# Rank order, rank widths and the last rank's evacuation in a fused cross-attention and mixture-of-experts kernel

## The chip, the cores and the metric

The kernel runs on one core of a Trainium2 chip. The metric is the device time of one execution in microseconds (us).

## What is computed

The input is 2048 tokens (4 x 512) of width 512, all in f32. The first half of the reference adds to each token a gated block chosen by its token id; the change doesn't touch it. The second half is a mixture of experts:

```python
logits = jnp.einsum('th,eh->te', x, gate_w)
topk_w, topk_ids = jax.lax.top_k(softmax(logits), K)       # K = 4 of E = 32
topk_w = topk_w / jnp.sum(topk_w, axis=-1, keepdims=True)
...
gu = jnp.einsum('ech,ehf->ecf', buf, w13)                  # 512 -> 2 x 256
g, u = jnp.split(gu, 2, axis=-1)
act = jax.nn.silu(g) * u
eo = jnp.einsum('eci,eih->ech', act, w2)                   # 256 -> 512
routed = jnp.zeros_like(x).at[tok].add(out_slots * flat_w[order][:, None])
...
out = residual + (routed + shared).reshape(B, S, Hd)
```

Here `x` is the normalised input, `buf` gathers the tokens of each expert, and `shared` is a further gated block that all tokens pass. An expert has 256 tokens on average; how many each one has follows from the data.

## The kernel before, in words

**Until about 257 us.** The tokens go through the first half in blocks of 128. Each token's row (512 values, 4 expert numbers, 4 weights, its own number) is scattered by GpSimd into a table in DRAM, `s_dram`, which has 320 slots for each expert. The shared block follows in four groups of 512 tokens (`glu_up` L848, `shared` L876); its results and the residual are put into `out` by GpSimd. Meanwhile `ranks()` (L791) counts the tokens of each expert and sorts the experts by count: rank 0 has the most. It also works out `over`: whether any expert has more tokens than its rank may have (`lim`, L827 to L841). If so, a slow branch after the loop (L1297) redoes the work; its condition is loaded by each engine at L1263.

**The expert loop (L1249 to L1293).** It runs over `ORDER`, a list of the 32 ranks written out by hand; I call a position in it a place, 0 to 31. Each place computes up to 256 tokens of its rank (`CM`). Ranks 0 to 5 may have 64 more tokens, ranks 6 to 17 may have 32 more; these extra rows of two ranks (64 each) or four ranks (32 each) are packed to 128 rows and computed together, as a block, at the place of the first of these ranks (0, 2, 4, 6, 10, 14). Ranks from `LOW` on compute fewer than 256 columns (`width`, L1057).

At a place:

- Sync's queue fetches rows three places ahead (`fetch` L961, `fetch_x` L970 for a block) and weights five places ahead (`weights` L921, six DMAs of 256 KB). There are six sets of weight buffers, so a place's weights may be loaded once the place six before is done with its own.
- DVE transposes the rows (L993) and scales them (L999, ACT L1003).
- `up_rank` (L1063) multiplies by `w13`: 16 matmuls whose moving operand is as wide as the rank, into `pg` and `pu`; then silu on ACT (L1076) and the product on DVE (L1079). Where a rank is narrower than 256, DVE sets the rest of `aT` to zero (L1087).
- If a block is due, `up_block` (L1154), `turn_block_act` (L1174) and `down_block` (L1182) run its matmuls, L1161, L1177 and L1188.
- `down_rank_by_halves` (L1098) multiplies by `w2` with seven products of halves (L1114) in place of eight. ACT (L1117) and DVE (L1120) weight and combine them into `eo`, two tiles of 128 rows. The last rank uses the plain `down_rank` (L1143) with `weighted` (L1035).
- `push` (L1040): GpSimd adds each tile of `eo` to the rows of `out` that its tokens own, by an indirect DMA that accumulates. The adds of one expert touch different rows and are declared free of each other. Two experts may share tokens, so the first add of a place waits until all adds of the place before have landed. A place whose rank has extra rows has a third add (`eo_x`).

At place 29 a drain is put into GpSimd's queue behind the adds of place 28 (L1259 to L1261). PSUM pools: `ps_o` and `ps_t` have two buffers each, `ps_m` three, `ps_s` one. `eo` has seven buffers.

The tile framework may interleave instructions of neighbouring places on PE: the up products of the next place run between the seven products of this one.

Of the kernel before, what the change touches and what calls it, by code (L numbers as in the profile page):

```python
# [8 lines left out]
F32 = mybir.dt.float32  # L9
I32 = mybir.dt.int32  # L10
U32 = mybir.dt.uint32
AF = mybir.ActivationFunctionType
ALU = mybir.AluOpType
AX = mybir.AxisListType
# [3 lines left out]
P = 128  # L18
T = 2048
D = 512  # L20
# [6 lines left out]
E = 32  # L27
K = 4
C = 2 * T * K // E
CM = 256  # L30
MJ = CM // P
I = 256
IC = I // P
# [4 lines left out]
XA, XWA = 6, 64  # L38
XZ, XWB = 18, 32
# [1 line left out]
NXA = XA // XPA  # L41
NX = NXA + (XZ - XA) // XPB

LOW = ((26, 240), (29, 228))


ORDER = (
    [0, 1, 2, 3, 18, 19]
    + [*range(6, 10), 20, 21, 4, 5, 22, 23]
    + [*range(10, 14), 24, 25]  # L50
    + [*range(14, 18), *range(26, E)]
)
SL = CM + XWA
NS = E * SL
# [12 lines left out]
def tile_xattn_moe(  # L67
# [15 lines left out]
    nc = tc.nc  # L83

    const = ctx.enter_context(tc.tile_pool(name="const", bufs=1))
# [3 lines left out]
    ps_t = ctx.enter_context(tc.tile_pool(name="ps_t", bufs=2, space=PSUM))  # L89
    ps_m = ctx.enter_context(tc.tile_pool(name="ps_m", bufs=3, space=PSUM))  # L90
    ps_o = ctx.enter_context(tc.tile_pool(name="ps_o", bufs=2, space=PSUM))
# [112 lines left out]
    def behind(ins, other, kind=mybir.DependencyClass.NoSync):  # L204

        tc.add_manual_dep(
            ins.ins,
            other.ins.name,
            mybir.DependencyInfo(kind, mybir.DependencyReason.DATA),
            reason="order",  # L210
        )
# [21 lines left out]
    n = EX * NT  # L233
# [546 lines left out]
    def base(j):  # L780
        return put_rows(out, xtok[:, j : j + 1], acc[:, j, :], out_puts, "base")
# [9 lines left out]
    def ranks():  # L791
        pn = ps_s.tile([P, E], F32, tag="sm", name="pn")
        nc.tensor.matmul(pn, ones16, before_[G], start=True, stop=True)
        n_e = slots.tile([P, E], F32, name="n_e")
        nc.vector.tensor_copy(n_e, pn)
        key = slots.tile([P, E], F32, name="key")
        nc.vector.scalar_tensor_tensor(key, n_e, float(E), iota_e, ALU.mult, ALU.subtract)
        grid = slots.tile([P, E, E], F32, tag="grid", name="grid")
        nc.vector.tensor_tensor(
            grid,  # L800
            key.unsqueeze(1).to_broadcast([P, E, E]),
            key.unsqueeze(2).to_broadcast([P, E, E]),
            ALU.is_gt,
        )
        rank = slots.tile([P, E], F32, name="rank")
        nc.vector.tensor_reduce(rank, grid, AX.X, ALU.add)

        def of(ranks_, n, name):

            pick = grid[:, :n, :]  # L810
            nc.vector.tensor_tensor(
                pick,
                ranks_.unsqueeze(2).to_broadcast([P, n, E]),
                rank.unsqueeze(1).to_broadcast([P, n, E]),
                ALU.is_equal,
            )
            nc.vector.tensor_tensor(pick, pick, iota_e.unsqueeze(1).to_broadcast([P, n, E]), ALU.mult)
            er = const.tile([P, n], F32, name=name)
            nc.vector.tensor_reduce(er, pick, AX.X, ALU.add)
            return er  # L820

        er = of(iota_e, E, "er")
        er_i = const.tile([P, E], I32, name="er_i")
        nc.vector.tensor_copy(er_i, er)
        er_x = of(rank_x, NX, "er_x")

        lim = slots.tile([P, E], F32, name="lim")  # L827
        more = slots.tile([P, E], F32, name="more")
        nc.vector.tensor_scalar(lim, rank, float(XA), float(XWA - XWB), ALU.is_lt, ALU.mult)
        nc.vector.tensor_scalar(more, rank, float(XZ), float(XWB), ALU.is_lt, ALU.mult)  # L830
        nc.vector.scalar_tensor_tensor(lim, lim, float(CM), more, ALU.add, ALU.add)
        had = CM
        for r, n in LOW:
            nc.vector.tensor_scalar(more, rank, float(r), float(had - n), ALU.is_ge, ALU.mult)
            nc.vector.tensor_tensor(lim, lim, more, ALU.subtract)
            had = n
        nc.vector.tensor_tensor(lim, n_e, lim, ALU.is_gt)
        over = slots.tile([P, 1], F32, name="over")
        nc.vector.tensor_reduce(over, lim, AX.X, ALU.add)
        over_i = const.tile([P, 1], I32, name="over_i")  # L840
        nc.vector.tensor_copy(over_i, over)  # L841
        return er, er_x, er_i, over_i


    HD = D // 2
    muls_s, adds_s = [], []

    def glu_up(xT, w13t, name):  # L848
        aT = cols.tile([P, IC, GT * P], F32, tag="aT", name=f"aT_{name}")
        for f in range(IC):  # L850
            pg = ps_m.tile([P, GT * P], F32, tag="mm", name="pg")
            pu = ps_m.tile([P, GT * P], F32, tag="mm", name="pu")
            for ps, fo in ((pg, f), (pu, IC + f)):
                for c in range(DC):
                    ins = nc.tensor.matmul(
                        ps, w13t[:, c, fo * P : (fo + 1) * P], xT[:, c, :], start=(c == 0), stop=(c == DC - 1)
                    )
                    if c % 2:
                        step(ins)
            if f == 0:  # L860
                first_half = ins
            s = mid.tile([P, GT * P], F32, tag="silu", name="s")
            nc.scalar.activation(s, pg, AF.Silu)
            muls_s.append(nc.vector.tensor_tensor(aT[:, f, :], s, pu, ALU.mult))
        return aT, first_half

    def glu_down(aT, w2t, i):
        po = ps_o.tile([P, D], F32, tag="po", name="po")
        for f in range(IC):
            ins = nc.tensor.matmul(  # L870
                po, aT[:, f, i * P : (i + 1) * P], w2t[:, f, :], start=(f == 0), stop=(f == IC - 1)
            )
        step(ins)
        return po

    def shared(g, aT):  # L876
        for i in range(GT):
            j = g * GT + i
            po = glu_down(aT, shw2, i)
            adds_s.append(nc.vector.tensor_tensor(acc[:, j, :], acc[:, j, :], po, ALU.add))  # L880
            to_put.append(lambda j=j: base(j))
# [27 lines left out]
    wts_a = ctx.enter_context(tc.tile_pool(name="wts_a", bufs=2))  # L909
    third = ctx.enter_context(ExitStack())  # L910
    slots = third.enter_context(tc.tile_pool(name="slots", bufs=1))
    er, er_x, er_i, over_i = ranks()
    for g in range(G):
        if g:
            aT_s[g], _ = glu_up(h2T[g], shw13, f"s{g}")
        shared(g, aT_s[g])
    while to_put:
        to_put.pop(0)()

# [113 lines left out]
    EO = 7  # L1033

    def weighted(po, wt, name, tag, m=P):  # L1035
        eo = last.tile([P, D], F32, tag=tag, name=f"eo_{name}", bufs=EO if tag == "eo" else 2)
        nc.scalar.mul(eo[:m, :], po[:m, :], wt[:m, :])
        return eo
# [18 lines left out]
    def width(r):  # L1057

        return min([CM] + [n for r_, n in LOW if r >= r_])

# [82 lines left out]
    def down_rank(aT, w2t, wt, to, n, r):  # L1143
        for j in range(MJ):
            m = min(P, n - j * P)
            po = ps_o.tile([P, D], F32, tag="po", name="po")
            for f in range(IC):
                nc.tensor.matmul(
                    po[:m, :], aT[:, f, j * P : j * P + m], w2t[:, f, :], start=(f == 0), stop=(f == IC - 1)
                )  # L1150
            eo = weighted(po, wt[:, j : j + 1], f"{r}_{j}", "eo", m)
            push(eo[:m, :], to[:m, j : j + 1], f"rank{r}")

    def up_block(xT, ws, name, after_=None, turned_=None):  # L1154
# [68 lines left out]
    wt = {r: weights(r) for r in ORDER[:2]}  # L1223
# [6 lines left out]
    last = ctx.enter_context(tc.tile_pool(name="last", bufs=1))  # L1230
# [18 lines left out]
    for i, r in enumerate(ORDER):  # L1249
# [14 lines left out]
        if q is not None:  # L1264
            xT_next, next_ = turn_parts(got[q][0], f"{q}", summed)
        R = w2_sums(wt[r][1], r) if r < E - 1 else None
        aT, made, last_up, wr = up_rank(
            xT,
            wt[r][0],
            width(r),  # L1270
            f"r{r}",
            next_,
            lambda first_: given(got[r][1], er[:, r : r + 1], f"{r}", first_),
        )
# [8 lines left out]
        if pend:  # L1283
            n, rs_, ws, a, xw, tox = pend
            aTx = turn_block_act(a, f"x{n}")
            eo = weighted(down_block(aTx, ws, last_up), xw[:, 0:1], f"x{n}", "eo_x")
            m = P // len(rs_)
# [8 lines left out]
    slots = ctx.enter_context(tc.tile_pool(name="slots_l", bufs=1))  # L1296
    with tc.If(need > 0):  # L1297
# [37 lines left out]
        for q in range(NT // NH):  # L1335
# [5 lines left out]
            for t in range(NH):  # L1341
                j = q * NH + t
# [4 lines left out]
            for e in range(E):  # L1347
                w = weights(e, e)
                for t in range(NH):
                    j, name = q * NH + t, f"l{q}_{e}_{t}"  # L1350
                    xw = given(of_l[:, t : t + 1, :], iota_e[:, e : e + 1], name)
                    a = up_block(rows_l[t], [w], name)
                    po = down_block(turn_block_act(a, name), [w])
# [7 lines left out]
                    eo = last.tile([P, D], F32, tag="eo", name=f"eo_{name}", bufs=EO)  # L1361
                    nc.scalar.copy(eo, po)
                    nc.vector.scalar_tensor_tensor(acc[:, j, :], eo, xw[:, 0:1], acc[:, j, :], ALU.mult, ALU.add)
                    po = ps_o.tile([P, D], F32, tag="po", name="po_l")
# [3 lines left out]
        for j in range(NT):  # L1368
            tp = ps_s.tile([P, P], F32, tag="sm", name="tp_l")
# [3 lines left out]
            po = ps_o.tile([P, D], F32, tag="po", name="po_l")  # L1373
# [4 lines left out]
        for i in range(NT):  # L1378
            nc.vector.tensor_scalar(row_l, xtok, float(-i * P), None, ALU.add)
            po = ps_o.tile([P, D], F32, tag="po", name="po")  # L1380
# [43 lines left out]
```

## Time and profile before

| what | us |
|---|---|
| median of 3 runs (lowest to highest) | 624.11 (622.13 to 624.48) |
| the profiled execution | 623.74 |
| its span | 621.9 |
| first up product of place 0 starts | 257.2 |
| last matmul of the last rank ends | 610.6 |
| last add issued by GpSimd | 614.6 |

A profile row has the line, the engine, the operation, the output and the inputs. A timeline row starts with its start and its length in us; in brackets at its end stand the engine's idle time before it and what ended that. A PE row counts records; each f32 matmul has two of them. The granted clock is 1.00 all through the expert loop. The code lines in the profile are those of the kernel before.

### The profile page before, as it was taken

The numbers are of one execution on the slowest core, as the hardware profiler recorded it, in microseconds if no ns is written. First come the engines' busy times: TensorE is split into PE (matmuls) and PEld (weight loads), VectorE is DVE, ScalarE is ACT, GpSimd is POOL, SyncE is SP. The second block draws the span as 40 slices with busy tenths as digits, with TensorE's granted clock in tenths as the row PEclk, the third lists the DMA queues.
The fourth block names the chain that finished last, engine by engine and source line by source line (L and its number), as shares of the span: only waits on it lengthen the run. The fifth ranks groups of instructions, "written<-read, shape, count | busy, mean of one in ns | idle before, by whom it ended". The sixth has DMA issues, their size and how long they took to land. (4 is left out here: it accounts for less than half of the span.)

```text
span 621.9 us, 10438 instructions
## 1 busy us (share of the span) xinstructions
PE 601.4 (97%) x2962; PEld 433.5 (70%) x2962; DVE 401.1 (65%) x1113; ACT 216.8 (35%) x390; POOL 248.6 (40%) x217
## 2 busy tenths in 40 slices
PE   5999999999999999999999999999999999999992
PEld 2777767777644444567786788768778886888881
DVE  7655456676548611766677677857867776787850
ACT  2445675756332000122233233333333333333330
POOL 4461002266677655332252343243323424243432
PEclk9999999999999999999999999999999999999997
DMA  7489993226365788699989997998999999999434
GB/s 252 155 310 396 414 413 154 104 105 224 122 249 198 271 323 240 211 320 285 306 169 277 281 226 171 293 247 180 253 273 277 193 219 296 264 250 227 52 40 57
DMA packets 104450, 144.55 MB, mean 232 GB/s; under 512 B 21184, under 2 KB 58048, under 8 KB 101824
## 3 DMA queue, kind: packets, MB, share of 16 engines
q1 hardware_dynamic: 86400, 101.54, 55.1%
q0 software_dynamic: 17984, 42.26, 28.1%
q8 instruction: 26, 0.43, 0.3%
q14 instruction: 40, 0.33, 0.2%
HBM read 79.05 MB, written 66.22 MB: 234 GB/s over the span
## 5 line engine op out<-in xcount | busy, mean ns | idle before, releaser
L1042 POOL DMA_INDIRECT out<-eo,to_all x64 | 101.5, 1587 | 221.0 <-DVE eo L1120 92.1
L1072 PE MATMUL pg<-xT,w 128*128 128x256 f32 (+2 forms) x512 | 135.4, 377 | 0.0
L1117 ACT ACTIVATE eo<-po,wt 128x256 f32<-128x256 f32 x124 | 58.6, 474 | 167.0 <-PE po L1114 147.0
L1072 PE MATMUL pu<-xT,w 128*128 128x256 f32 (+2 forms) x512 | 114.0, 376 | 0.0
L1072 PEld LDWEIGHTS pg<-xT,w 128*128 128x128 f32 x512 | 96.6, 190 | 18.5 <-issue 6.2
L1072 PEld LDWEIGHTS pu<-xT,w 128*128 128x128 f32 x512 | 97.3, 190 | 11.5
L652 POOL DMA_INDIRECT s_dram<-h,slot x64 | 64.1, 1002 | 24.4 <-issue 15.2
L464 PEld LDWEIGHTS pp<-xT,held 128*128 128x128 f32 x576 | 66.8, 192 | 7.4 <-issue 5.7
L464 PE MATMUL pp<-xT,held 128*128 128x128 f32 x576 | 68.2, 276 | 0.6 <-DVE st_b L611 0.6
L485 PE MATMUL po<-cT,aT 128*128 (+1 forms) x152 | 68.4, 592 | 0.0
L993 DVE STREAM_TRANSPOSE xT<-z 128x1024 f32<-128x1024 f32 x32 | 65.1, 2034 | 0.0
L1120 DVE SCALAR_TENSOR_TENSOR eo<-po,wt,eo 128x256 f32<-128x256 f32 x93 | 44.9, 484 | 24.6 <-PE po L1114 19.6
L1079 DVE TENSOR_TENSOR aT_r<-s,pu 128x256 f32<-128x256 f32 (+2 forms) x64 | 26.5, 414 | 39.0 <-PE pu L1072 37.1
L485 PEld LDWEIGHTS po<-cT,aT 128*128 128x128 f32 x152 | 27.4, 190 | 27.3 <-issue 27.3
L1003 ACT ACTIVATE xT<-xT,nwq 128x256 f32<-128x256 f32 x64 | 29.0, 500 | 46.2 <-DVE xT L993 45.2
L618 POOL TENSOR_TENSOR rs<-rs,mhalf 128x2 f32<-128x2 f32 x16 | 11.3, 705 | 72.7 <-DVE rs L617 72.7
L1095 DVE TENSOR_TENSOR t_r<-w,t_r 128x256 f32<-128x256 f32 x62 | 26.4, 426 | 21.0 <-PE po L1114 20.4
L395 ACT COPY held<-cT 128x1024 f32 x36 | 36.0, 1047 | 10.2 <-DVE valid L312 10.0
L1114 PE MATMUL po<-w,aT_r 128*128 128x256 f32 x124 | 37.8, 386 | 0.1
L1114 PE MATMUL po<-t_r,s_r 128*128 128x256 f32 x124 | 37.6, 385 | 0.0
L1114 PE MATMUL po<-t_r,aT_r 128*128 128x256 f32 x124 | 37.3, 382 | 0.0
L870 PE MATMUL po<-shw,aT_s 128*128 128x512 f32 x64 | 29.6, 602 | 0.3 <-DVE acc L880 0.3
(203 smaller groups left out, 763.5 us busy)
## 6 DMA issues: line engine op xcount, KB each, us to landing
w<-in_w SPq DMA_DIRECT2D x192, 256.0 KB
s_dram<-none SPq DMA_DIRECT2D x1, 20840.0 KB
z<-s_dram SPq DMA_DIRECT2D x128, 128.0 KB
h_dram<-h SPq DMA_DIRECT2D x4, 1042.0 KB
cT<-in_ctxT SPq DMA_DIRECT2D x4, 1024.0 KB
out<-none SPq DMA_DIRECT2D x1, 1024.0 KB
s_dram<-h,slot POOLq DMA_INDIRECT x64, 3.3
out<-eo,to_all POOLq DMA_INDIRECT x64, 7.3
```

The lines of the kernel that those rows point to most:

```text
L395: ins = nc.scalar.copy(held[b][:, h : h + n], cT[:, bass.ds(e, 1), h : h + n].rearrange("p o c f -> p (o c) f"))
L464: ins = nc.tensor.matmul(ups[b][:, f, :], held[b][:, c, f * P : (f + 1) * P], xT_[b][:, c, :], start=(f == 0 and c == 0) if b == 0 else (c ...
L485: ins = nc.tensor.matmul(po, aT_[b][:, f, :], cT[:, bass.ds(off[b], 1), f, :].rearrange("p o f -> p (o f)"), start=(f == 0), stop=(f == DC ...
L652: put = nc.gpsimd.indirect_dma_start(out=table, out_offset=bass.IndirectOffsetOnAxis(ap=index, axis=0), in_=src, in_offset=None,)
L870: ins = nc.tensor.matmul(po, aT[:, f, i * P : (i + 1) * P], w2t[:, f, :], start=(f == 0), stop=(f == IC - 1))
L993: ins = nc.vector.transpose(xT.rearrange("p c (r b) -> p r c b", b=SQ), z.rearrange("p r (a c) -> p r c a", c=DC))
L1003: on_act.append(nc.scalar.mul(xT[:, c, :], xT[:, c, :], nwq[:, c : c + 1]))
L1042: put = nc.gpsimd.indirect_dma_start(out=out, out_offset=bass.IndirectOffsetOnAxis(ap=dst, axis=0), in_=eo, in_offset=None, bounds_check=T ...
L1072: last_up = nc.tensor.matmul(ps, w13t[:, c, f * P : (f + 1) * P], xT[:, c, :n], start=(c == 0), stop=(c == DC - 1))
L1114: return nc.tensor.matmul(ps, L[i], R[i], start=first_, stop=True, skip_group_check=True)
L1117: nc.scalar.mul(eo[i][:, j, :], ps, wt[:, i : i + 1])
L1120: return nc.vector.scalar_tensor_tensor(eo[i][:, j, :], ps, wt[:, i : i + 1], eo[i][:, j, :], ALU.mult, ALU.add)
```

## The change

It has four parts. `LOW` gets more entries: ranks 20 to 25 become narrower than 256 and ranks 28, 30 and 31 narrower than they were. `ORDER` moves ranks 4 and 5, with the block of their extra rows, from places 12 and 13 to 28 and 29; the later ranks of the middle move up. The limits are worked out by a function of their own, behind the adds of the shared block's group 1. The last rank's results are computed in two column halves, each in a PSUM bank of its own, from `ps_o` for the first 128 rows and from `ps_t` for the others; ACT weights the first half and DVE the second.

| places | 0 to 5 | 6 to 9 | 10 to 13 | 14 to 17 | 18 to 21 | 22 to 25 | 26 to 31 |
|---|---|---|---|---|---|---|---|
| before | 0 1 2 3 18 19 | 6 7 8 9 | 20 21 4 5 | 22 23 10 11 | 12 13 24 25 | 14 15 16 17 | 26 27 28 29 30 31 |
| after | 0 1 2 3 18 19 | 6 7 8 9 | 20 21 22 23 | 10 11 12 13 | 24 25 26 14 | 15 16 17 27 | 28 29 4 5 30 31 |

```diff
-LOW = ((26, 240), (29, 228))
+LOW = ((20, 252), (22, 248), (24, 244), (26, 240), (28, 234), (29, 228), (30, 224))
...
     [0, 1, 2, 3, 18, 19]
-    + [*range(6, 10), 20, 21, 4, 5, 22, 23]
-    + [*range(10, 14), 24, 25]
-    + [*range(14, 18), *range(26, E)]
+    + [*range(6, 10), *range(20, 24)]
+    + [*range(10, 14), *range(24, 27)]
+    + [*range(14, 18), *range(27, 30)]
+    + [4, 5, 30, 31]
...
-        lim = slots.tile([P, E], F32, name="lim")
...
-        return er, er_x, er_i, over_i
+        def limits(after_):
+
+            lim = slots.tile([P, E], F32, name="lim")
+            more = slots.tile([P, E], F32, name="more")
+            behind(
+                nc.vector.tensor_scalar(lim, rank, float(XA), float(XWA - XWB), ALU.is_lt, ALU.mult), after_
+            )
...
+            return over_i
+
+        return er, er_x, er_i, limits
...
-    er, er_x, er_i, over_i = ranks()
+    er, er_x, er_i, limits = ranks()
...
         shared(g, aT_s[g])
+        if g == 1:
+            over_i = limits(adds_s[-1])
...
     def down_rank(aT, w2t, wt, to, n, r):
         for j in range(MJ):
             m = min(P, n - j * P)
-            po = ps_o.tile([P, D], F32, tag="po", name="po")
-            for f in range(IC):
-                nc.tensor.matmul(
-                    po[:m, :], aT[:, f, j * P : j * P + m], w2t[:, f, :], start=(f == 0), stop=(f == IC - 1)
-                )
-            eo = weighted(po, wt[:, j : j + 1], f"{r}_{j}", "eo", m)
+            banks, tag = ((ps_o, "po"), (ps_t, "tp"))[j % 2]
+            eo = last.tile([P, D], F32, tag="eo", name=f"eo_{r}_{j}", bufs=EO)
+            for h in range(2):
+                of = slice(h * HD, (h + 1) * HD)
+                po = banks.tile([P, HD], F32, tag=tag, name="po")
+                for f in range(IC):
+                    nc.tensor.matmul(
+                        po[:m, :], aT[:, f, j * P : j * P + m], w2t[:, f, of], start=(f == 0), stop=(f == IC - 1)
+                    )
+                if h:
+                    nc.vector.tensor_scalar(eo[:m, of], po[:m, :], wt[:m, j : j + 1], None, ALU.mult)
+                else:
+                    nc.scalar.mul(eo[:m, of], po[:m, :], wt[:m, j : j + 1])
             push(eo[:m, :], to[:m, j : j + 1], f"rank{r}")
```

More of the change, by code (lines that the diff above doesn't have):

```diff
@@ L825, in ranks @@
         er_x = of(rank_x, NX, "er_x")
-        lim = slots.tile([P, E], F32, name="lim")
[L828 to L841, printed above, removed]
-        return er, er_x, er_i, over_i
+        def limits(after_):
[4 more added lines that the diff above has]
+            )
+            nc.vector.tensor_scalar(more, rank, float(XZ), float(XWB), ALU.is_lt, ALU.mult)
+            nc.vector.scalar_tensor_tensor(lim, lim, float(CM), more, ALU.add, ALU.add)
+            had = CM
+            for r, n in LOW:
+                nc.vector.tensor_scalar(more, rank, float(r), float(had - n), ALU.is_ge, ALU.mult)
+                nc.vector.tensor_tensor(lim, lim, more, ALU.subtract)
+                had = n
+            nc.vector.tensor_tensor(lim, n_e, lim, ALU.is_gt)
+            over = slots.tile([P, 1], F32, name="over")
+            nc.vector.tensor_reduce(over, lim, AX.X, ALU.add)
+            over_i = const.tile([P, 1], I32, name="over_i")
+            nc.vector.tensor_copy(over_i, over)
+            return over_i
+        return er, er_x, er_i, limits
     HD = D // 2
```

## The prediction

> **What bounds the kernel now.** I read the page's busy shares first, then the stretches of the expert loop, then what PE waited for, then GpSimd's timeline.
>
> The page, and the stretches of the expert loop (columns: us, then busy of PE, PEld, DVE, ACT and POOL, granted clock, DMA share, GB/s):
>
> ```profile
> PE 601.4 (97%) x2962; PEld 433.5 (70%) x2962; DVE 401.1 (65%) x1113; ACT 216.8 (35%) x390; POOL 248.6 (40%) x217
> ```
>
> ```profile
> 433.00:480.00 47.00, 47.00 (x241) 36.15 (x240) 34.33 (x82) 14.41 (x30) 15.47 (x10) 1.00 1.11 269
> 522.00:570.00 48.00, 48.00 (x234) 40.01 (x234) 35.80 (x87) 15.99 (x33) 18.92 (x13) 1.00 1.08 262
> 570.00:611.00 41.00, 40.59 (x190) 33.91 (x188) 26.37 (x70) 13.53 (x28) 15.12 (x10) 1.00 0.51 67
> ```
>
> PE is busy without a gap from 257.2 to 610.6 us at full clock, so TensorE work taken off the loop shortens it one for one. The DMA engines are full as well, until about 570 us, when the last weights are in; then their share halves. PE's waits in the loop are 0.3 us at most. But PE's end isn't the kernel's end: 11.3 us follow. The timeline says why:
>
> ```profile
> 392.01 1.55 POOL L1042 DMA_INDIRECT out<-eo,to_all  x1 [5.85 <-DVE wt L1022]
> 393.86 1.55 POOL L1042 DMA_INDIRECT out<-eo,to_all  x1 [0.30 <-ACT eo L1117]
> 403.02 1.69 POOL L1042 DMA_INDIRECT out<-eo,to_all  x1 [7.61 <-DVE xT L993]
> 405.02 1.55 POOL L1042 DMA_INDIRECT out<-eo,to_all  x1 [0.30 <-issue]
> 413.32 1.55 POOL L1042 DMA_INDIRECT out<-eo,to_all  x1 [6.75 <-DMA out<-eo,to_all]
> ...
> 604.35 1.55 POOL L1042 DMA_INDIRECT out<-eo,to_all  x1 [4.23 <-DMA out<-eo,to_all]
> 606.20 1.56 POOL L1042 DMA_INDIRECT out<-eo,to_all  x1 [0.30 <-issue]
> 612.74 1.56 POOL L1042 DMA_INDIRECT out<-eo,to_all  x1 [4.98 <-DVEq L1297]
> ```
>
> ```profile
> 608.91 0.69 ACT L1037 ACTIVATE eo<-po,wt 128x512 f32<-128x512 f32 x1 [4.18 <-PE po L1148]
> ```
>
> An expert's adds into `out` (two, three where a rank has extra rows) start only when all adds of the expert before have landed. I call it the chain. The last rank's first half is ready at 608.91 + 0.69 = 609.60, but its add starts at 612.74: it waits for the landing of the add issued at 606.20. (The releaser named, L1297, is the If after the loop, which gives an add nothing: the landing came last.) From that start to the end of the span: 621.9 - 612.74 = 9.16 us.
>
> So there are two clocks. **PE**: the first half of a place's results is ready (end of its second L1120) at 376.4, 386.4, 396.7 for places 9 to 11, hence 10.0 and 10.3 a place; where a block begins, 13.2 to 13.7 (396.7 to 410.4), then 12.4. **Chain**: a step is the time from a place's first add to the next place's. Steps that the chain itself set: with two adds 11.0, 10.3, 10.8, 10.9 (from places 10, 11, 14, 20), mean 10.75; with three 11.7, 11.0, 11.5, 11.1, 10.7, 11.4, 11.4 (from 8, 9, 12, 18, 19, 24, 25), mean 11.25. After 570 us, two adds: 8.3, 8.7, 10.25 (that one holds the drain of L1261), 7.65, 8.4. So while weights are being loaded the chain is slower than PE on a plain place; it falls behind (6.3 us at place 11) and catches up where a block gives PE 6 us more. Place 12 is such a catch-up: the delay goes 6.3, 2.9, 2.1, 0.6.
>
> **The change, part by part.**
>
> *Narrower ranks.* Columns saved: ranks 20, 21: 4 each; 22, 23: 8; 24, 25: 12; 28: 6; 30, 31: 4; together 62. Price: sixteen L1072 `pu` records last 3.62 us at 256 columns and 3.24 at 228: 0.38 / (16 x 28) = 0.85 ns a column and record, 32 records a place: 27 ns a column. 62 x 27 ns = **-1.7 us** of PE. The counts that the reference's routing gives are inside the new limits (247 at rank 20 against 252, 239 at 25 against 244, 201 at 30 against 224), so the overflow branch stays untaken. Six more memsets on DVE (L1087, 105 ns) stand ahead of the sums s1 to s4; PE runs the next rank's up products meanwhile, as it did at places 26 to 30: 0; without that cover 6 x 0.1 = 0.6 us.
>
> *The limits moved behind group 1's adds.* Nineteen small DVE operations of about 0.2 us, 3.7 us from 215.9, in an idle stretch that lasts until 222.10 (L864, waiting 6.25 us for PE). Sync's load of `over_i`, 217.7 before, moves to about 220; what is queued behind it (the first `z`) went at 231.96, waiting for scatters. 0 on both; the cover is 2.5 us and 11 us. What they leave on DVE (204 to 208 us) had no waiter on PE.
>
> *Column halves for the last rank.* Two matmul halves to two banks, ACT takes one (0.47, L1117) and DVE the other (no such row; the nearest are 0.42, L1079, and 0.48, L1120) in place of one ACTIVATE of 0.69. That is 0.2 us per row block at most, and 0 while the chain is late: the landing ends last there. Against it, the second matmul needs `aT`'s second half after 0.43 us and not 0.86: it comes at 607.58, PE asks at 607.42, 0.2 us. I take 0 for both; -0.7 to +0.2 are the ends.
>
> *Ranks 4 and 5 at places 28 and 29.* PE's work of the block, 3.65 (L1161) + 0.38 + 1.94 (L1188), about 6 us, moves and doesn't change. Sync's fetch of its rows (10.3 us of queue at 373) moves to the fetch for place 28. Weights reach their buffers when place p-6 frees them, as now; the block of ranks 10 to 13 wants place 17's weights at about 423 us, and by today's Sync cadence (9.4 us a place) they are there by 414: 0. What counts is the chain. It loses its catch-up at place 12, and gets three adds at 28 and 29, with the drain behind place 28's. Up to its first add of place 10 (392.0, delay 5.7) nothing changes. PE's time between places is 10.0, less 27 ns for each column taken off, 13.3 into a place with a block and 12.4 out of it. I take 10.6 for two adds under load (between 10.3 and 11.0; three of the four rows stand in Sync's catching up after a block fetch) and 11.3 for three (rows 10.7 to 11.7):
>
> - 10 to 14: 4 x 10.6 = 42.4, PE 43.2, delay 5.7 to 4.9
> - 14 to 21: 4 x 11.3 + 3 x 10.6 = 77.0, PE 75.0: 6.9
> - 21 to 26: 4 x 11.3 + 10.6 = 55.8, PE 51.4: 11.3
> - 26 to 27, loads ending: 9.4 (between 8.3 and 10.6); 27 to 28: 8.4
> - 28 to 29: three adds and the drain: 10.25 + 1.87 for the third issue, less some 0.5 because the third is small: 11.6 (ends 10.5, 12.1)
> - 29 to 30, three adds, quiet: 8.0 + 1.87 - 0.3 = 9.6 (ends 8.4, 10.3); 30 to 31: 8.2
>
> First add of the last rank: 392.0 + 42.4 + 77.0 + 55.8 + 9.4 + 8.4 + 11.6 + 9.6 + 8.2 = 614.4, against 612.74. Span 614.4 + 9.2 = 623.6. The profiled execution took 623.74 for a span of 621.9, 1.84 around it: **625.4 us**. That execution is 0.37 below the median 624.11; I add nothing for it, as the three runs shown differ by 2.35. The gain on PE is lost because PE's end no longer decides anything.
>
> **The rivals.**
>
> *The chain keeps up* (faster). If the loaded steps are 0.3 shorter (10.3 and 11.0; sixteen steps, 4.8 us), place 28, where PE needs 13.2 against the chain's 8.4, clears the delay and PE decides: it ends at 610.6 - 1.7 = 608.9; the first half of place 29 is ready 18.0 before that; its add starts at 590.9 + 0.6, place 30's 9.6 later, the last one's 8.2 later at 609.3: span 618.5, time 620.3. For it: a fetch less around 380 us, landings of 5 us when the queues are quiet. Against it: the landings under load (median 7.8 us from 480 to 570, the waits by tile), which don't depend on the order. The Trainium skill ("DMA: Bandwidth & Descriptors", Anatomy of one DMA) gives a DMA issued from GpSimd about 2.0 us and its bytes at 436 GB/s, which for 256 KB would be an estimated 2.6 us; by that the chain would never be late and this rival would hold. No landing here is under 4.4 us, and by the trace the rule does not carry over to adds beside other loads.
>
> *The chain is slower still* (slower). The place is the sixteen loaded steps between 392 and 567 us, where an add queues behind Sync's weight loads; the price is 16 x 0.1 = 1.6 us for each 0.1 us of mean step. At 10.9 and 11.5 the sum gains 8 x 0.3 + 8 x 0.2 = 4.0: 629.4. It passes 0.5% (627.2) from a mean of 0.11 above mine, and the plain mean of the rows is 10.75. Against: Sync's loads should be less bunched without the fetch at 373.
>
> *It doesn't do what it says*: the halves' separate banks shorten nothing. That is part of the forecast; only the first rival makes them worth up to 0.7.
>
> **How the numbers follow.** Chain late, near today's steps: 0.44, 625.4. Chain keeps up: 0.27, 620.3. Chain slower: 0.29, 629.4. Range: 619.5 to 629.5, from the first rival to the second; the forecast's own is 621 to 627.2. About 0.5% is what a measurement of this kernel tells from no change (621.0 to 627.2): faster 0.27, same 0.44, slower 0.29.
>
> **What would show it.** The sixteen `pu` records at rank 24 should last 0.16 us less; PE should end near 609 with no new wait. The first add of place 14 should come about 5 us after its result, that of place 26 about 11 us, that of place 28 about 6; the last rank's first add at 614 with its result ready at 608. If the delay at place 28 is under 1 us, the first rival holds; if it is over 9 us, the second. A PE gap over 1 us at places 14, 21 or 28 (weights) would make all three wrong.

## The result, and the profile after

Changed kernel: **620.49 us**, median of 7 runs (618.94 to 620.72); before, beside it: 623.23, median of 7 (621.54 to 624.48). Ratio **0.9951**, 95% interval 0.9932 to 0.9969. The prediction was 625.4. The time is close to that of its first rival, "the chain keeps up" (620.3).

In the lines below, code lines of the changed kernel are shifted: the up products are L1081, the products of halves L1123, the adds L1051, the last rank's products L1161, its two halves L1167 (ACT) and L1165 (DVE). First the page's busy times and the three stretches of the loop:

```profile
PE 600.2 (97%) x2970; PEld 434.3 (70%) x2970; DVE 405.1 (65%) x1131; ACT 216.2 (35%) x390; POOL 249.3 (40%) x217
```

```profile
433.00:480.00 47.00, 47.00 (x225) 39.90 (x218) 34.40 (x88) 16.00 (x33) 19.24 (x13) 1.00 1.00 242
522.00:570.00 48.00, 48.00 (x230) 41.63 (x229) 37.47 (x95) 15.96 (x33) 17.22 (x13) 1.00 0.97 232
570.00:611.00 41.00, 40.21 (x188) 30.65 (x187) 24.65 (x64) 11.85 (x25) 15.90 (x11) 1.00 0.42 51
```

PE is as full as before, at full clock, and the DMA engines are nearly as full until 570 us (242 and 232 GB/s after 269 and 262). The averages don't show what changed; GpSimd's timeline does. The adds of places 10 to 12, and of places 30 and 31:

```profile
391.73 1.56 POOL L1051 DMA_INDIRECT out<-eo,to_all  x1 [5.62 <-DMA out<-eo_x,to_x]
393.60 1.56 POOL L1051 DMA_INDIRECT out<-eo,to_all  x1 [0.30 <-issue]
400.38 1.56 POOL L1051 DMA_INDIRECT out<-eo,to_all  x1 [5.22 <-DVE t_r L1104]
402.24 1.56 POOL L1051 DMA_INDIRECT out<-eo,to_all  x1 [0.30 <-ACT xT L1012]
409.27 1.56 POOL L1051 DMA_INDIRECT out<-eo,to_all  x1 [5.46 <-DMA out<-eo,to_all]
...
602.98 1.56 POOL L1051 DMA_INDIRECT out<-eo,to_all  x1 [5.11 <-DVE eo L1129]
604.85 1.56 POOL L1051 DMA_INDIRECT out<-eo,to_all  x1 [0.30 <-ACT s L1085]
610.45 1.57 POOL L1051 DMA_INDIRECT out<-eo,to_all  x1 [4.04 <-ACT eo L1167]
612.33 1.45 POOL L1051 DMA_INDIRECT out<-eo,to_all  x1 [0.31 <-issue]
```

A step is the distance between first adds: 400.38 - 391.73 = 8.65 and 409.27 - 400.38 = 8.89, where I had put 10.6. When was the last rank's first result ready, and when did PE end? DVE's and PE's timelines:

```profile
608.65 0.48 DVE L1165 TENSOR_SCALAR eo<-po,wt 128x256 f32<-128x256 f32 x1 [1.26 <-PE po L1161]
```

```profile
606.73 3.62 PE L1161 MATMUL po<-w,aT_r 128*128 128x256 f32 x16
```

Ready at 608.65 + 0.48 = 609.13, added from 610.45: 1.32 behind, where before had 3.14. PE ends at 606.73 + 3.62 = 610.35.

The two profiled spans, 621.9 and 618.9, can be accounted for piece by piece:

| piece | before | after | difference |
|---|---|---|---|
| first up product of place 0 starts | 257.21 | 258.39 | +1.18 |
| from there to PE's end | 353.38 | 351.96 | -1.42 |
| PE's end to the last rank's first add | +2.15 | +0.10 | -2.05 |
| first to second add | 1.87 | 1.88 | +0.01 |
| second add to the end of the span | 7.29 | 6.57 | -0.72 |

The first row is the first half of the kernel, which the change doesn't touch but for the limits; between profiles on one chip it varied by up to 1.5 us. The experiments ask which of the others come back.

### The profile page after: what moved, and what is told of

The parts are those of the page before. It is cut to its first block, busy times and chain, and to the rows that moved or that the text cites. A ratio compares the mean times of both kernels' runs of the same rounds, so it can differ in the third digit from the quotient of the medians.

```text
span 618.9 us, 10478 instructions
## 1 busy us (share of the span) xinstructions
PE 600.2 (97%) x2970; PEld 434.3 (70%) x2970; DVE 405.1 (65%) x1131; ACT 216.2 (35%) x390; POOL 249.3 (40%) x217
## 4 chain that ended last, share of the span: by engine, by line
PE 75%; POOL 7%; issue 6%; DMA 5%; DVE 4%; SPq 2%; POOLq 0%; ACT 0%; DVEq 0%; ACTq 0%
PE pg L1081 18%; PE pu L1081 17%; PE po L1123 16%; PE pp L465 5%; PE po L486 4%; POOL s_dram L653 4%; PE pp_x L1177 3%; DMA acc<-in_x,xtok 3%; PE pg L862 3%; PE pu L862 3%; PE po L877 3%; PE po L1204 2%; SPq L949 2%; POOL acc L333 1%; POOL rs L619 1%
## 5 line engine op out<-in xcount | busy, mean ns | idle before, releaser
L1051 POOL DMA_INDIRECT out<-eo,to_all x64 | 102.2, 1598 | 217.0 <-DVE eo L1129 95.7
L1081 PE MATMUL pg<-xT,w 128*128 128x256 f32 (+7 forms) x512 | 135.0, 375 | 0.0
L1081 PE MATMUL pu<-xT,w 128*128 128x256 f32 (+7 forms) x512 | 113.1, 374 | 0.0
L1081 PEld LDWEIGHTS pg<-xT,w 128*128 128x128 f32 x512 | 96.6, 190 | 18.2 <-issue 6.2
L1081 PEld LDWEIGHTS pu<-xT,w 128*128 128x128 f32 x512 | 97.3, 190 | 10.7
L1088 DVE TENSOR_TENSOR aT_r<-s,pu 128x256 f32<-128x256 f32 (+7 forms) x64 | 26.4, 412 | 37.2 <-PE pu L1081 35.5
L619 POOL TENSOR_TENSOR rs<-rs,mhalf 128x2 f32<-128x2 f32 x16 | 11.3, 706 | 72.7 <-DVE rs L618 72.6
L396 ACT COPY held<-cT 128x1024 f32 x36 | 36.0, 1046 | 10.3 <-DVE valid L313 10.0
L1123 PE MATMUL po<-w,aT_r 128*128 128x256 f32 x124 | 37.8, 387 | 0.1
L1123 PE MATMUL po<-t_r,s_r 128*128 128x256 f32 x124 | 37.6, 385 | 0.0
L1123 PE MATMUL po<-t_r,aT_r 128*128 128x256 f32 x124 | 37.4, 383 | 0.0
```

The lines of the kernel that those rows point to most:

```text
L396: ins = nc.scalar.copy(held[b][:, h : h + n], cT[:, bass.ds(e, 1), h : h + n].rearrange("p o c f -> p (o c) f"))
L1051: put = nc.gpsimd.indirect_dma_start(out=out, out_offset=bass.IndirectOffsetOnAxis(ap=dst, axis=0), in_=eo, in_offset=None, bounds_check=T ...
L1081: last_up = nc.tensor.matmul(ps, w13t[:, c, f * P : (f + 1) * P], xT[:, c, :n], start=(c == 0), stop=(c == DC - 1))
L1123: return nc.tensor.matmul(ps, L[i], R[i], start=first_, stop=True, skip_group_check=True)
```

## Experiments

They ran on several chips. On most of them the first half takes some 9 us longer (mean granted clock 0.99 after 0.995), so each ratio is to the kernel before on the same chip. The delay of a place is its first add's start less its result; 0.3 is its floor.

### One part at a time

Theory A here: the new order shortens the chain. Theory B: the narrower ranks do it.

**order_only**: the new `ORDER`, the rest as before.

> The kernel before with the new rank order alone. Theory A (the order shortens the chain of adds: without the fetch of ranks 4 and 5's extra rows in the middle, the adds of the places 10 to 12 meet fewer weight loads): the two-add steps from places 10, 11 and 12 are about 9.0 us (after: 8.65, 8.89, 9.01) and not 10.3 to 11.0, the delay is cleared by place 14 and again at place 28, and the time falls by 2.0 to 2.7 us although no PE work goes. Theory B (the narrower ranks made the chain keep up, by moving the adds against the weight loads): the steps from 10 to 12 stay at 10.3 to 11.0, the delay at place 26 is over 8 us, and the time is 0 to 3 us above the kernel before.

Measured: 0.9987 (0.9975 to 1.0000), 0.8 us. The steps from places 10 to 12 were 8.3, 9.6 and 10.1, shorter than in before, as theory A has it; but the time fell by less than half of its 2.0 us. The delay at places 26 and 27 was 5.3 and 5.2 (theory B: over 8), and 0.3 at places 28 to 30.

**low_only**: the new `LOW`, the rest as before.

> The kernel before with the narrower ranks alone. PE saves 62 columns x 27 ns = 1.7 us. Theory A: the chain still ends the kernel; 48 of the 62 columns lie ahead of place 22, where PE last sets the pace, so about 1.3 us of it reach the end, and the steps from 10 and 11 stay near 11.0 and 10.3. Theory B: the steps from 10 and 11 fall to about 9 us, the last add waits for its result, and the time falls by 2.5 us or more.

Measured: 0.9972 (0.9958 to 0.9987), 1.8 us. PE's loop 351.94. The steps from 10 and 11 were 10.1 and 10.8. The delay was 0.4 to 1.5 at places 28 to 30, and the last rank's first add started 0.27 behind its result: PE's gain came through with the old order, where my sum let none of it reach the end and theory A 1.3 us. Neither theory holds: the order does shorten the chain, but the end did not wait for the chain here.

**halves_only**: the column halves alone.

> The kernel before with the last rank in column halves alone. By the prediction 0: the last rank's first add still waits for the landing of place 30's adds (612.7 us against a result that is ready at about 609.3). Rival: the adds wait for the result after all, and the time falls by 0.4 to 0.7 us.

Measured: 0.9998 (0.9985 to 1.0011).

**limits_only**: the limits behind group 1's adds, alone.

> The kernel before with the limits worked out behind the adds of the shared block's group 1, alone (two entries, so nine operations and not nineteen). Expected 0 by both theories: DVE waits there for PE. If the later start of the expert loop in the changed kernel (258.55 against 257.21 us) comes from this part, the loop starts 1.3 us later here too and the time rises by about 1 us.

Measured: 0.9997 (0.9984 to 1.0009). Both as forecast: nothing. But halves_only gave nothing for another reason than mine: its last rank's first add did not wait for the landing (the delay at place 30 was 0.3), so the rival's condition was met. Its 0.4 to 0.7 us did not show: that first add started 0.45 before PE's end, in limits_only, with one piece, 0.72.

The three profiles here with the order of before differ from the one in my prediction: the delay at place 30 is 0.3 or 0.4, not 2.6.

### How far steps vary, and the row fetch

**before_again, after_again**: both kernels unchanged, profiled once more.

> The kernel before, profiled once more, beside itself. Theory A (the loaded steps are set by the order of the places, so they come back in every execution): two-add steps at places 10, 11 again 11.0 and 10.3, three-add steps 10.7 to 11.7, mean 11.25, delay at place 11 about 6, tail from PE's end to the span's end 11.3. Theory B (the loaded steps vary from one execution to another by more than the 0.3 that I had between forecast and rival): three-add steps 10.3 to 10.8, delay at place 11 about 3, at places 29 and 30 under 2, tail under 10.5. Ratio 1.000 in both, within 0.002.

> The changed kernel, profiled once more. Both theories: ratio 0.996 (0.994 to 0.998). Theory A: two-add steps at places 10, 11, 12 again 8.7, 8.9, 9.0, delay at place 13 about 1. Theory B: any of these steps may be 10 or more, but the delay at places 28 and 29 is under 1 us in any case, since place 28 with its block gives the chain over 13 us; tail about 8.6.

Measured: 0.9996 (0.9985 to 1.0007) and 0.9964 (0.9951 to 0.9977). GpSimd's, ACT's and PE's timelines of before_again at the end:

```profile
612.02 1.55 POOL L1042 DMA_INDIRECT out<-eo,to_all  x1 [3.86 <-DVE eo L1120]
614.04 1.56 POOL L1042 DMA_INDIRECT out<-eo,to_all  x1 [0.47 <-ACT eo L1117]
619.82 1.56 POOL L1042 DMA_INDIRECT out<-eo,to_all  x1 [4.22 <-ACT eo L1037]
621.69 1.63 POOL L1042 DMA_INDIRECT out<-eo,to_all  x1 [0.30 <-issue]
```

```profile
618.86 0.69 ACT L1037 ACTIVATE eo<-po,wt 128x512 f32<-128x512 f32 x1 [4.19 <-PE po L1148]
```

```profile
616.94 3.60 PE L1148 MATMUL po<-w,aT_r 128*128 128x512 f32 x8
```

The result is ready at 618.86 + 0.69 = 619.55 and its add starts 0.27 later, 0.72 before PE's end at 620.54. The same program, yet the wait of 3.14 us that carried my prediction is not there. Of seven profiles with the order of before, only the one I read had it.

In after_again two-add steps were 8.2 to 12.2: 10.55, 8.75 and 12.10 from places 10, 11 and 12. So a step is not fixed by its place, as theory A had it; theory B holds.

**light_fetch**: the block's eight row loads become one.

```diff
+        if rs_[0] == 4:
+            load(z.rearrange("p a b -> p (a b)"), w2[0, :P, :])
```

> The kernel before with the row loads of the block of ranks 4 and 5 (eight row gathers) replaced by one plain load of 256 KB from the weights: the block's rows are other data, so that part of the computation is left out. Sync's queue is then hardly held at 373 to 383. Theory A (Sync's catching up after this fetch is what lengthened the steps at places 10 and 11, and moving the block away is what shortened them): steps at places 10 and 11 fall from 10.2 to 11.0 down to 8.3 to 9.6, delay at place 12 under 1; time equal to that of before within 0.8 us, since the block at place 12 clears the delay anyway. Theory B (the fetch has nothing to do with it): steps at 10 and 11 stay at 10.2 to 11.0.

**extra_fetch**: the changed kernel with one more block fetch.

```diff
+        if i == 9:
+            fetch_x(range(4, 6), "again")
```

> The changed kernel with a second fetch of the extra rows of ranks 4 and 5, which nothing uses, put into Sync's queue at place 9, about where before has it. Theory A: steps at places 10 to 12 rise from 8.7 to 10.1 up to 10.2 to 11.0, delay at place 13 about 3 to 5, cleared at place 14 by its block; time that of the changed kernel within 0.6 us, ratio 0.996 to before. Theory B: steps and delays as in the changed kernel.

Measured: 1.0001 (0.9991 to 1.0010) and 0.9991 (0.9970 to 1.0012). First adds of places 10 to 12, light_fetch and then extra_fetch, on GpSimd's timeline:

```profile
400.71 1.55 POOL L1046 DMA_INDIRECT out<-eo,to_all  x1 [6.62 <-DVE ws L1020]
...
411.45 1.55 POOL L1046 DMA_INDIRECT out<-eo,to_all  x1 [7.20 <-DVE xT L1003]
...
422.13 1.62 POOL L1046 DMA_INDIRECT out<-eo,to_all  x1 [7.27 <-DVE t_r L1099]
```

```profile
400.70 1.56 POOL L1051 DMA_INDIRECT out<-eo,to_all  x1 [5.30 <-DMA out<-eo_x,to_x]
...
410.85 1.56 POOL L1051 DMA_INDIRECT out<-eo,to_all  x1 [6.73 <-DMA out<-eo,to_all]
...
419.10 1.56 POOL L1051 DMA_INDIRECT out<-eo,to_all  x1 [4.82 <-DVE t_r L1104]
```

Without the fetch 10.7 and 10.7 (theory A: 8.3 to 9.6), with it 10.15 and 8.25 (theory A: 10.2 to 11.0). That this one fetch made the steps long, which I had reasoned in the prediction, is not borne out; with one profile each, and steps that vary as above, it is not ruled out either. extra_fetch took 629.53 us beside 628.51 for after_again; 0.77 of it is in PE's loop (352.73), and I don't know why.

What the traces do show is the load beside a step. Sync's timeline of the changed kernel's first profile, around the step from place 11 (400.38, 8.89 us long):

```profile
387.21 5.18 SPq L949 DMA_DIRECT2D w<-in_w  x6
392.77 0.65 SPq L949 DMA_DIRECT2D z_x<-s_dram  x1
...
400.93 0.32 SPq L949 DMA_DIRECT2D num_x<-s_dram  x1
401.44 2.00 SPq L949 DMA_DIRECT2D z<-s_dram  x4
403.69 0.40 SPq L949 DMA_DIRECT2D of<-s_dram  x1
404.33 3.20 SPq L949 DMA_DIRECT2D w<-in_w  x6
```

From 392.4 to 404.3 Sync issues no weights, only rows, most of them those of the block of place 14. In the first 8 us of that step its queue moved 0.91 MB; in the first 8 us of before's step from place 10 (11.0 us long) 1.70 MB. Take all two-add steps between places 8 and 25 that the chain itself set. With ranks 4 and 5 at places 28 and 29 (eight profiles) 23 steps had less than 1.2 MB and lasted 8.9 us in the mean; 37 had more and lasted 10.7. With the order of before (six profiles) all 22 had more, and lasted 10.6. Of the 23, 19 are at places 11, 18 and 25, three ahead of the blocks at 14, 21 and 28, where the rows of a block are fetched. In the order of before the stretches with less fall at places 9, 13 and 19, which have three adds, and there three-add steps show no such difference (10.7 with less, 10.8 with more). This compares profiles; no experiment held the load alone.

### What the chain costs in all

Theory A now: the chain is late at the end in a usual execution, and my profile was typical. Theory B: it was not.

**two_tables, two_tables_a**: before and after, with every second place adding into another table.

```diff
+        odd = group is not None and ORDER.index(int(group[4:])) % 2
...
-            out=out,
+            out=out_b if odd else out,
```

> The kernel before, with the adds of every second place put into a second table in DRAM, so that an expert's adds wait for those two places back and never for the place just before; these rows are left out of the result. It measures what the chain costs in all. Theory A (in a usual execution the chain is late at the end, as in the one profile from which I summed, where the last rank's first add began 2.15 us behind PE's end): the last first add moves to about 0.7 before PE's end, time 2 to 3 us below before, ratio 0.9955. Theory B (that one execution was out of the ordinary; usually the chain has caught up by the last rank, and its first add begins 0.7 before PE's end already): time 0 to 0.9 us below before, ratio 0.9985 to 1.000.

> The changed kernel with the same second table for every second place (these rows are left out of the result). The last rank's first half is ready 1.2 us before PE's end, and its add starts 0.45 before PE's end in the second profile of the changed kernel; without the chain it should start 0.9 before it. Theory B: 0 to 0.5 us below the changed kernel, ratio to before 0.9955 to 0.9965. Theory A: as the changed kernel or up to 2 us below it (0.993).

Measured: 1.0005 (0.9996 to 1.0014) and 0.9984 (0.9975 to 0.9993). In both, the first add of nearly every place starts 0.28 us behind its result: the chain is gone. The time of before didn't fall at all. GpSimd's and ACT's timelines of two_tables:

```profile
610.89 1.56 POOL L1044 DMA_INDIRECT out_b<-eo,to_all  x1 [4.22 <-ACT eo L1038]
612.75 1.63 POOL L1044 DMA_INDIRECT out_b<-eo,to_all  x1 [0.30 <-issue]
```

```profile
609.93 0.69 ACT L1038 ACTIVATE eo<-po,wt 128x512 f32<-128x512 f32 x1 [4.19 <-PE po L1150]
```

The add is 0.27 behind the result, just as in before_again with its chain. Theory B holds, on this chip. (From its last add to the end of the span two_tables takes 7.35 us, 0.4 above the mean with one table, below; that much of a gain could be hidden.) two_tables_a missed its number: its last first add is 0.46 before PE's end, as with the chain, but from the last add to the end of the span it takes 7.51 us instead of 5.97 to 6.58; the table has a cost of its own there, which I didn't follow up.

**earlier**: ranks 4 and 5 two places earlier. **no_drain**: the changed kernel without the drain.

```diff
-    + [*range(14, 18), *range(27, 30)]
-    + [4, 5, 30, 31]
+    + [*range(14, 18)]
+    + [27, 4, 5, 28, 29, 30, 31]
```

```diff
-        if i == E - 3:
-            with queued(adds[f"rank{ORDER[i - 1]}"]):
-                nc.gpsimd.drain()
```

> The changed kernel with ranks 4 and 5 at places 26 and 27 and ranks 28 and 29 at 28 and 29. The chain then has two more places behind the three-add ones to catch up. Theory B: delay at place 26 is 0.3, at 29 and 30 at most 1; the last first add 0.7 to 0.9 before PE's end; time equal to the changed kernel or 0.5 below, ratio 0.995 to 0.997. Theory A: 1 to 2 us below the changed kernel, 0.994.

> The changed kernel without the drain in GpSimd's queue behind the adds of place 28. Step from place 28 to 29 stays at 12.4, since PE sets it there; what the drain took from the end of the kernel may come back: Theory B 0 to +0.5 us against the changed kernel. Theory A: the chain is shorter by up to 1.8, ratio to before 0.994.

Measured: 0.9975 (0.9966 to 0.9985) and 1.0010 (1.0001 to 1.0019). Without the drain the kernel is 620.6 x 0.0035 = 2.2 us slower than `earlier`, beside it on the same chip; the two also differ in the order of the last six places, which makes no difference in the next runs. Neither theory had that. The changed kernel did not run on this chip; `earlier`, 1.6 us below before, is just outside what I expected (0.995 to 0.997). GpSimd's last add and the span of no_drain, and of after_three (below):

```profile
610.75 1.45 POOL L1051 DMA_INDIRECT out<-eo,to_all  x1 [0.31 <-issue]
```

```profile
core 0: 619.5 us, clock 0.995
```

```profile
620.05 1.45 POOL L1051 DMA_INDIRECT out<-eo,to_all  x1 [0.30 <-issue]
```

```profile
core 0: 626.2 us, clock 0.993
```

619.5 - 610.75 = 8.75 us from the last add to the end, against 6.15. In no_drain the last add's packets end 4.0 us ahead of the span's end, in the other profiles with one table 1.8 to 2.15. GpSimd's own drain at the kernel's end lasts 7.40 us in no_drain (L1433, from 611.29), until 3.2 us past the last of these packets; in after_three 4.59 us (L1436, from 620.49), until 0.7 past it.

### Where the rest of the gain lies

**after_three, earlier_two**: the changed kernel and `earlier`, side by side. **rows_96**: before, with `(30, 224)` added to `LOW`.

> The changed kernel again, on the chip of the two runs sent with it. PE's loop is 351.96 us as in both profiles so far, the tail from PE's end 8.0 to 8.6; ratio to before 0.996 (0.995 to 0.9975). If the order itself were worth nothing and only PE's 1.43 us counted, the ratio would be 0.9977.

> Ranks 4 and 5 at places 26 and 27, beside the changed kernel on the same chip. Theory B (the chain has caught up in both, PE decides): equal to the changed kernel within 0.5 us. Theory A (the chain still sets the end in the changed kernel): 1 to 2 us below it.

> The kernel before with ranks 30 and 31 at 224 columns instead of 228, and nothing else: the last add of all then has 96 rows and not 100. PE is 8 columns x 27 ns = 0.2 us shorter. In the profiles so far the packets of the last add took 5.0 to 5.2 us with 100 rows (323 packets) and 3.9 to 6.1, mean 4.6, with 96 (260 packets): if that is the rows' doing, another 0.4 us, ratio 0.999; if it is chance, ratio 0.9997.

Measured: 0.9962 (0.9948 to 0.9975), 0.9965 (0.9952 to 0.9979) and 0.9991 (0.9981 to 1.0000). The place of ranks 4 and 5 within the last six makes no difference. In rows_96 the last add starts at

```profile
621.60 1.44 POOL L1042 DMA_INDIRECT out<-eo,to_all  x1 [0.30 <-issue]
```

on GpSimd's timeline, and the span ends at 627.9: 6.30 us. Over all profiles with one table and the drain, this piece is 6.72 to 7.29 with 100 rows in the last add (six profiles, mean 6.98) and 5.97 to 6.58 with 96 (ten, mean 6.30). The two don't overlap: 0.7 us for four rows.

**no_halves**: the changed kernel with the last rank's results in one piece, and **after_four** beside it.

> The changed kernel with the last rank's results in one piece again. In every profile with the halves the last rank's first add starts 0.76 us or more behind its result and 0.45 before PE's end (it waits for two engines); with one piece 0.27 behind and 0.72 before. Expected: first add 0.72 before PE's end, the second 1.87 later, tail 0.27 shorter than in the changed kernel; loop 351.98; time 0.3 us below it, which its interval can't tell, ratio to before 0.9957 (0.9945 to 0.997). If the halves are worth what they shorten on ACT and DVE, the first add starts later than 0.72 before PE's end and the time is 0.2 us above.

> The changed kernel beside the run without halves, on the same chip: ratio to before 0.996 (0.995 to 0.9975), loop 351.98, last rank's first add 0.45 before PE's end if the chain has caught up, later if not; last add to the span's end 6.0 to 6.6.

Measured: 0.9952 (0.9935 to 0.9970) and 0.9958 (0.9946 to 0.9971); the times don't tell the two apart. no_halves' first add of the last rank, with its result on ACT:

```profile
617.71 1.57 POOL L1051 DMA_INDIRECT out<-eo,to_all  x1 [4.35 <-ACT eo L1046]
```

```profile
616.54 0.69 ACT L1046 ACTIVATE eo<-po,wt 128x512 f32<-128x512 f32 x1 [4.14 <-PE po L1157]
```

It is 0.52 before PE's end at 618.23, not 0.72: by the chain of waits place 30's last add landed at 616.93, and the add started 0.78 behind that. In after_four the chain was late at the end, as it was, by 0.6 us, in the first profile of the changed kernel; first adds of places 27 to 31 on GpSimd's timeline:

```profile
582.50 1.56 POOL L1051 DMA_INDIRECT out<-eo,to_all  x1 [8.17 <-DVE aT_r L1088]
...
590.77 1.56 POOL L1051 DMA_INDIRECT out<-eo,to_all  x1 [4.84 <-DVE t_r L1104]
...
602.48 1.55 POOL L1051 DMA_INDIRECT out<-eo,to_all  x1 [6.05 <-DVE eo L1129]
...
611.86 1.56 POOL L1051 DMA_INDIRECT out<-eo,to_all  x1 [4.17 <-DMA out<-eo_x,to_x]
...
619.68 1.57 POOL L1051 DMA_INDIRECT out<-eo,to_all  x1 [4.40 <-DVE eo L1165]
```

Their results were ready at 574.9, 588.6, 600.9, 610.2 and 617.77: delays of 7.6, 2.2, 1.6, 1.6 and 1.9. Place 28 with its block clears 7.6 - 2.2 = 5.4 of a delay; what is more reaches the end.

## Why the prediction was wrong

- **The failed step** is the term "10.6 for two adds under load" (and, less, 11.3 for three), set against PE's 10.0. In the eight profiles with ranks 4 and 5 at places 28 and 29, the two-add steps between places 8 and 25 that the chain itself set are 8.1 to 12.3, mean 9.98 (60 steps); the three-add ones 9.8 to 12.7, mean 10.96 (69). From place 10 to 26 I summed 42.4 + 77.0 + 55.8 = 175.2 us for the chain. The changed kernel's four profiles give 168.2, 168.2, 166.7 and 169.9, where PE needs 169.0. The chain keeps pace; the delay at place 26 was 2.3 to 5.5, not 11.3, and place 28 cleared it (0.3) in three of the four and left 2.2 in after_four.
- **Why 10.6 didn't carry over.** In six profiles with the order of before the mean is 10.62 (22 steps): the size was right for that order, and it is right in the new one where Sync's queue is as full (10.7). The prediction put it on every two-add step up to about 570 us, and argued that the landings under load "don't depend on the order". But the order changes which steps are loaded: in the new one 23 of 60 met fewer loads, most of them while Sync fetched a block's rows, and took 8.9 us. That steps and loads go together is shown across profiles; that the load is the cause is argued. For three adds the prediction's list also left out the steps from places 13, 17 and 23 (8.9, 11.1 and 11.9), which the chain set too; the mean of all ten is 11.06, not 11.25.
- **The base was one execution**, and an unusual one. Its delay of 3.14 at the last rank, from which "PE's end no longer decides anything" followed, came back in none of six further profiles with that order. Even the sum's start was off: the first add of place 10 began 134.8 us after place 0's first up product in before, 133.3 in the changed kernel (132.6 to 135.2 in its other three profiles), though the order is the same until there. two_tables shows the chain's price on another chip: none.
- **The first rival** had the mechanism right: place 28 "clears the delay and PE decides". It asked for steps of 10.3 and 11.0 and a last first add at 609.3, with PE's end at 608.9; measured 9.98 and 10.96, 610.45 and 610.35, in a loop that began 1.2 us later. That its time fits to 0.2 us is partly luck: most of the late start was made up by the piece from the last rank's first add to the end, 8.45 us in place of 9.2, which it did not foresee. Its ground by the Trainium skill ("DMA: Bandwidth & Descriptors", Anatomy of one DMA), an estimated 2.6 us for 256 KB, was not the reason. By the chain of waits the second add of place 30 lands 4.5 to 5.2 us after issue with the queues almost empty (5.78 in the profile that I read), and the chain keeps up all the same.
- **PE -1.7**: 1.42, and 1.43 in low_only. A column is worth 1.43 / 62 = 23 ns, not 27. The `pu` records shorten as forecast (3.62 to 3.56 us for 4 columns); the rest of a place gives less, which I didn't resolve.
- **Limits 0, halves 0**: no effect in their ratios, 0.13% to either side. But at the end the halves lose a little. Their first add starts 0.45 before PE's end where the chain isn't late, that of one piece 0.72. The result comes 0.2 us sooner (1.21 before PE's end, after 0.99), and the add starts 0.76 behind it instead of 0.27, which fits GpSimd having two engines to wait for.
- **Left out**: that a narrower last rank shortens the last add, 0.7 us.

Together -1.43 - 0.7 + 0.27 = -1.9 us, which the profiles show as means where the chain isn't late at the end. The four comparisons of the changed kernel give ratios of 0.9951 to 0.9964, or 2.3 to 3.1 us. What remains, 0.4 to 1.2 us, fits the chain being late in some executions of before (order_only: -0.8 us, with an interval that reaches no change), but single runs without a profile can't show it: that part is argued, not shown. On the chip of two_tables, where the chain had no price, nothing remains: `earlier` gains 1.6 us (0.9 to 2.1).

## What to carry to other kernels

A wait at the end of one profiled execution may be chance: before summing sixteen steps of it, look whether its chain and the engine beside it run at nearly the same pace (here 10.6 against 10.0), for then a few per cent in a step turn the outcome. Price a step by the transfers that run beside it, and ask whether the change moves them too. Where two clocks run side by side, price the faster case with the engine's own saving, and look for the place that lets the slower one catch up. At the end of a kernel, the size of the very last transfer counts in full, and a hand-over from two engines can cost more (0.5 us here) than dividing the work saves (0.2).

## What the runs showed of the hardware

- The same step of the same program varied between executions by up to 3 us (in the changed kernel's four profiles 9.0 to 12.1 from place 12, 8.2 to 9.9 from place 25), while PE's loop agreed within 0.1 us (351.94 to 352.01, apart from 352.73 in extra_fetch).
- Four rows less in the last indirect add, 96 after 100, bring the end 0.7 us nearer; the trace has 256 packets of its queue for it after 320.
- A two-add step of the chain took 8.9 us in the mean where Sync's queue moved less than 1.2 MB in its first 8 us (23 steps), and 10.6 to 10.7 where it moved more (59).
- A drain in GpSimd's queue three places before the end, hidden behind a place where PE takes 12.4 us anyway, saves 2.2 us at the end; GpSimd's closing drain lasts 4.59 us with it (after_three) and 7.40 without.
